# A two-layer graph network on one core: source one-hots by ScalarE and VectorE in three of seven chunks, and one gathered bucket of seven instead of two

## The chip, the cores and the metric

One core of a Trainium2 chip runs the whole program. The metric is the device time of one execution in microseconds (us). Below, PE is TensorE's matmul path, PEld its weight load, DVE is VectorE, ACT is ScalarE, POOL is GpSimd and SP is SyncE, whose queue issues most of the plain DMAs.

## What is computed

There are 6250 nodes with 128 channels and 200,000 edges (`src`, `dst`), sorted by `dst`. Two attention layers follow each other, and each adds its result to its input and normalizes the rows:

```python
hij = concat([h[src], h[dst]], axis=-1)                       # layer 0
exp_e = exp(leaky_relu(hij @ w, 0.2) @ a)
out = segment_sum(h[src] * exp_e / segment_sum(exp_e, src)[src], dst)
x = layernorm(x + out)

s = leaky(H_s[:, src] + H_t[:, dst]); s = exp(s - max(s))     # layer 1, 4 heads
agg = segment_sum(s / (segment_sum(s, src)[src] + 1e-8) * H[dst], src)
x = layernorm(x + elu(agg + x @ residual_projection))
```

## The kernel before

**Buckets.** The nodes are cut into 49 blocks of 128. Every edge lies in one of 49 x 49 buckets, by its destination's block j and its source's block i, and a bucket has 128 slots. For a bucket the kernel keeps, slot by slot, the edge's source and destination inside their blocks: as columns (`cols`, slots on partitions) and as rows in DRAM (`rows_jm`, `rows_im`). A row of numbers that is copied to all 128 partitions and compared with the partition's number gives a one-hot matrix, nodes by slots; a matmul with it as the weights reads a block's table rows out into the slots (a gather). The transposed matrix, slots by nodes, sums slots back into nodes. Buckets are worked off in chunks of seven, so a row of 49 buckets has seven chunks, c = 0 to 6. The engines run freely, each in the order of its own queue as the program writes it; they wait for each other through buffers and data.

**Stage A, `score_edges`, up to about 1520 us.** For each destination block j: while row j is scored, the slots of row j+3 are found (`find_slots`, a generator whose steps are interleaved by `find_more`, one step of each running generator after each chunk). `score_chunk` (L817) does one chunk. SP fetches the number rows of chunk k+3 (L806). DVE makes the one-hots of chunk k+2 (`one_hot`, L813, both kinds in one instruction). PE gathers the tables of both ends in 42 matmuls (L834) into PSUM tiles named `u` of three buckets each, of which there are four. DVE turns each bucket into one score per edge (L844, two instructions for a bucket). Then PE turns the seven one-hots of the sources (L850), and ACT copies the result from PSUM to `oh` (L852). Ten such `oh` tiles are kept: one row later, after chunk 1, `sums` (L790) uses the row's seven for the softmax's denominators. After chunk 6, ACT and DVE take the row's exponentials and split them into bf16 parts (`split3`, L476 to L480), in turns. Of `find_slots`, the prediction names the one-hot of the high digits (L666, read by PE at L673), the running counts (L682 and L684, which also use `u` tiles), the comparison at L723, the slot matmuls (L736), and L745, the first DVE step after them.

**Loading the ids.** `load_ids` (L599) reads the window of the edge list in which block j's edges lie, in two indirect DMAs from POOL's queue, whose row numbers are column j of `window_row`. One call stands after chunk 3 of each row, and eleven in the start-up. `split_ids` (L620) takes a group of seven of them apart on DVE.

**Stage B, the first part of `bucketed`, about 1540 to 2510 us.** It forms layer 0's sums, a row j at a time, each chunk in two groups of three and four buckets (`CUT`). Of a group's buckets, PE gathers those for which `by_dma` says no (L1289, three bf16 matmuls a bucket, from an exact split into three bf16 parts), and ACT copies them from PSUM (L1298). The others, the last `GP` of each chunk's seven in all rows but the first, come by indirect DMA from a table in DRAM (L1106, `Gathers`, POOL's queue, five chunks ahead). DVE makes the weighted one-hots (L1304, one a bucket), and PE sums them (L1320, f32; the profile counts two for each). `OneHots` fetches and converts (L1002) only the rows that PE needs. Each time seven rows are done, `nodes` is started: it normalizes these seven blocks and makes layer 1's tables, interleaved with the groups. Its writes (L1200, L1201) stand in SP's queue before later fetches of rows.

**Stage C, the second part, about 2535 to 3580 us.** It does the same for layer 1, a source block i at a time: L1367 and L1368 are the scores of the next row, L1419 the gather on PE, L1106 again the indirect DMA, L1436 the weighting (DVE, one instruction for the part from PSUM and one for the part from the DMA), L1443 the one-hots (DVE), L1457 the sums (PE). The scores need the one-hots of all seven buckets, so nothing is left out of their making. A tail (residual, elu, normalization, output) ends the program.

A second routine, `any_edges`, serves inputs that do not fit the slots; it does not run here.

Of the kernel before, what the change touches and what calls it, by code (L numbers as in the profile page):

```python
# [10 lines left out]
BF16 = mybir.dt.bfloat16  # L11
I32 = mybir.dt.int32
AF = mybir.ActivationFunctionType
OP = mybir.AluOpType
AX = mybir.AxisListType

P = 128
# [456 lines left out]
def split3(nc, pool, hi, mid, lo, v, shape, name):  # L474

    nc.scalar.activation(hi, v, AF.Copy)  # L476
    r = pool.tile(shape, F32, name=name)
    nc.vector.tensor_tensor(r, v, hi, op=OP.subtract)
    nc.scalar.activation(mid, r, AF.Copy)
    nc.vector.tensor_tensor(lo, r, mid, op=OP.subtract)  # L480


def score_edges(tc, keep, x, src, dst, w0, a0, rows_jm, rows_im):
# [4 lines left out]
    nc = tc.nc  # L488
    N, C = x.shape
    (E,) = src.shape  # L490
    NB = -(-N // P)
# [6 lines left out]
    CH = 7  # L498
    chunks = [(c, min(c + CH, NB)) for c in range(0, NB, CH)]
    NC = len(chunks)  # L500
    AHEAD = 3


    BEGIN, FIRST = (7, 16, 25, 35), 23
# [6 lines left out]
    cols = keep.tile([P, NB, 2, NB], BF16, name="cols")  # L511
# [3 lines left out]
    with ExitStack() as pools:  # L515
        fc = pools.enter_context(tc.tile_pool(name="fc", bufs=1))
# [3 lines left out]
        fa = pools.enter_context(tc.tile_pool(name="fa", bufs=2))  # L520
        fb = pools.enter_context(tc.tile_pool(name="fb", bufs=2, space=bass.MemoryType.PSUM))
        ft = pools.enter_context(tc.tile_pool(name="ft", bufs=2, space=bass.MemoryType.PSUM))
# [3 lines left out]
        nc.gpsimd.iota(iota_i, pattern=[[1, P]], base=1, channel_multiplier=0)  # L526
        iota_1 = fc.tile([P, P], BF16, name="iota_1")
        nc.vector.tensor_copy(iota_1, iota_i)
        part_i = fc.tile([P, 1], I32, name="part_i")
        nc.gpsimd.iota(part_i, pattern=[[0, 1]], base=0, channel_multiplier=1)  # L530
        part_f = fc.tile([P, 1], F32, name="part_f")
# [8 lines left out]
        ident_b = fc.tile([P, P], BF16, name="ident_b")  # L540
# [21 lines left out]
        window_row = fc.tile([P, NB], I32, name="window_row")  # L562
# [36 lines left out]
        def load_ids():  # L599

            j = len(loaded_ids)
            if j == NB:
                return
            b = next(b for b, (c0, c1) in enumerate(id_groups) if c0 <= j < c1)
            c0, c1 = id_groups[b]
            if j == c0:
                ids[b] = [fi.tile([P, CH, WT], I32, name=f"ids{k}") for k in range(2)]
            for to, flat in zip(ids[b], (src, dst)):
                if j == NB - 1:
                    nc.sync.dma_start(to[:, j - c0, :], flat[E - WT * P :].rearrange("(p t) -> p t", t=WT))  # L610
                    continue
                nc.gpsimd.indirect_dma_start(  # L612
                    out=to[:, j - c0, :],
                    out_offset=None,
                    in_=flat[: NR * WT].rearrange("(r t) -> r t", t=WT),
                    in_offset=bass.IndirectOffsetOnAxis(ap=window_row[:, j : j + 1], axis=0),
                )
            loaded_ids.append(j)

# [167 lines left out]
        def sums(j, ohs, ex3):  # L787
            dp = fb.tile([P, 3 * NB], F32, name="sm")
            for i in range(NB):
                nc.tensor.matmul(dp[:, 3 * i : 3 * i + 3], ohs[i // CH][:, i % CH, :], ex3[:, i, :], start=True, stop=True)  # L790
            if j == 0:
                nc.vector.tensor_copy(den, dp)
            else:
                nc.vector.tensor_tensor(den, den, dp, op=OP.add)
# [4 lines left out]
        def fetch(k):  # L799
            if k < len(order):  # L800
                j, c = order[k]
                c0, c1 = chunks[c]
                loaded[k] = ra.tile([P, 2, CH, P], BF16, name="rows")
                for w in range(2):
                    r = rows_jm[j, w, c0:c1].rearrange("r s -> (r s)")
                    nc.sync.dma_start(  # L806
                        loaded[k][:, w, : c1 - c0].rearrange(flat2), r[None, :].to_broadcast([P, (c1 - c0) * P])
                    )

        def one_hot(k):  # L810
            if k < len(order):
                rows = loaded[k].rearrange("p w i s -> p (w i s)")
                nc.vector.tensor_scalar(rows, rows, part_f, None, op0=OP.is_equal)  # L813

        state = {}

        def score_chunk(k):  # L817
            j, c = order[k]
            if c == 0:
                state["acc"] = wa.tile([P, NB], F32, name="acc")  # L820
                state["ohs"] = []
            acc, ohs = state["acc"], state["ohs"]
            fetch(k + 3)
            one_hot(k + 2)
            rows = loaded.pop(k)
            c0, c1 = chunks[c]
            for i0 in range(c0, c1, 3):
                n = min(3, c1 - i0)
                u = pa[0].tile([P, 512], F32, name="u")[:, : 3 * CX].rearrange("p (n c) -> p n c", c=CX)
                for d in range(n):  # L830
                    i = i0 + d
                    for w, b in ((0, i), (1, j)):
                        for s in range(3):
                            nc.tensor.matmul(  # L834
                                u[:, d, :],
                                rows[:, w, i - c0, :],
                                pq3[:, b, w, s, :],
                                start=(w == 0 and s == 0),
                                stop=(w == 1 and s == 2),
                            )  # L840
                for d in range(n):
                    i = i0 + d
                    junk = wa.tile([P, CX], BF16, name="junk")
                    nc.vector.scalar_tensor_tensor(  # L844
                        junk, u[:, d, :], 0.0, a_ext, op0=OP.max, op1=OP.mult, accum_out=acc[:, i : i + 1]
                    )

            tp = ft.tile([P, CH, P], BF16, name="tp")
            for i in range(c0, c1):
                nc.tensor.transpose(tp[:, i - c0, :], rows[:, 0, i - c0, :], ident_b)  # L850
            oh = woh.tile([P, CH, P], BF16, name="oh")
            nc.scalar.activation(oh[:, : c1 - c0], tp[:, : c1 - c0], AF.Copy)  # L852
            ohs.append(oh)
            if c == 1 and "late" in state:
                sums(*state["late"])
            if c + 1 == NC:
                nc.scalar.activation(ex[:, j, :], acc, AF.Exp, scale=1.0 - ALPHA)
                ex3 = wa.tile([P, NB, 3], BF16, name="ex3")
                split3(nc, wa, ex3[:, :, 0], ex3[:, :, 1], ex3[:, :, 2], ex[:, j, :], [P, NB], "exr")
                state["late"] = (j, ohs, ex3)  # L860
# [3 lines left out]
        with tc.tile_pool(name="n0", bufs=3) as n0:  # L864

            def tables(b, xt):
                mm = pa[0].tile([P, 512], F32, name="u")[:, : 2 * CX].rearrange("p (w c) -> p w c", c=CX)
                nc.tensor.matmul(mm, xt, w0_sb, start=True, stop=True)
                split3(nc, n0, pq3[:, b, :, 0, :], pq3[:, b, :, 1, :], pq3[:, b, :, 2, :], mm, [P, 2, CX], "pqr")
# [17 lines left out]
            for b in range(NB):  # L887
# [3 lines left out]
                tp = pa[0].tile([P, 512], F32, name="u")[:, :P]  # L891
# [23 lines left out]
            tables(*turned.pop(0))  # L915
            assert begun == len(BEGIN) == AHEAD + 1

        for k in range(scored, len(order)):
            j, c = order[k]
            if c == 0 and j > 0:  # L920
                if j + AHEAD < NB:
                    finding.append(find_slots(j + AHEAD))
                elif j + 1 == NB:
                    finding.append(check_slots())
            score_chunk(k)
            find_more()
            if c == 3:
                load_ids()
# [6 lines left out]
def bucketed(ctx, tc, x, w1, al, ar, wr, out, cols, ex, den, rows_jm, rows_im):  # L935
    nc = tc.nc
# [4 lines left out]
    NB = -(-N // P)  # L941
    LAST = N - (NB - 1) * P
    CD = C + H
    CH = 7
# [114 lines left out]


    CUT = 3
    GP = 2
    BY_PE = CH - GP
    assert NB % CH == 0

# [7 lines left out]
    class Gathers:  # L1073


        def __init__(self, pool, table, which, ahead, width):
            self.pool, self.table, self.ahead, self.width = pool, table, ahead, width
            base_i = consts.tile([P, NC, GP], I32, name=f"base_i{which}")
            nc.gpsimd.iota(base_i, pattern=[[CH * P, NC], [P, GP]], base=BY_PE * P, channel_multiplier=0)
            base = consts.tile([P, NC, GP], F32, name=f"base{which}")  # L1080
            nc.vector.tensor_copy(base, base_i)

            self.ids = consts.tile([P, NB, NC, GP], I32, name=f"ids{which}")
            for q in range(GP):
                if which == 0:
# [588 lines left out]
```

## Time and profile before

| | |
|---|---|
| median of 10 runs | 3642.73 us (3636.48 to 3644.98) |
| the profiled execution | 3637.54 us, of which the profile's span is 3635.7 us |
| PE busy | 3365.6 us, 93% |
| PEld busy | 3226.2 us, 89% |
| DVE busy | 3175.4 us, 87% |
| ACT busy | 2027.8 us, 56% |
| POOL busy | 1500.7 us, 41% |
| mean granted TensorE clock | 0.969 |

A group's line gives the line of code, the engine, the operation, the tiles (out<-in), the shape, the count, the busy time, the mean duration in ns and the idle time before it. Durations of neighbours overlap by some 0.1 us, so that the distance from one start to the next is the better price. A timeline's line gives the start and the duration in us and merges like instructions that follow each other; a bracket is the engine's idle time and who ended it.

### The profile page before, as it was taken

The page shows a single profiled execution, that of the slowest core. Times are in us where ns is not written, and L with a number is a line of the kernel's source. Part 1 is how long each engine was busy: PE and PEld are TensorE (multiplying, and loading weights), DVE is VectorE, ACT ScalarE, POOL GpSimd, SP SyncE. Part 2 cuts the span into 40 slices and gives each one's busy share as a digit, 9 for nine tenths or more (in the row PEclk, how much of TensorE's full clock was granted, in tenths as well). Part 3 has the DMA queues.
Part 4 walks back from the last instruction along what each step waited for, and adds up shares of the span by engine and source line. Part 5 has one row for each costly group of instructions (what it writes and reads, how often), then busy time and mean ns, then how long its engine had stood idle before and what let it go on. Part 6 is the DMA issues. An engine that isn't in the chain of part 4 may idle for free.

```text
span 3635.7 us, 125212 instructions
## 1 busy us (share of the span) xinstructions
PE 3365.6 (93%) x50166; PEld 3226.2 (89%) x50166; DVE 3175.4 (87%) x11723; ACT 2027.8 (56%) x3036; POOL 1500.7 (41%) x1474
## 2 busy tenths in 40 slices
PE   4699999999999999799999999997999999999996
PEld 3598989898989899788988988987999999999996
DVE  5588888888888888798888888887999999999997
ACT  4556666666666666343333333334666666666665
POOL 4001010101000000157766766764567676777771
PEclk6799999999999999899999999998999999999998
DMA  2133343333444433454544544445666666666672
GB/s 62 37 118 121 121 117 122 116 124 118 121 116 121 116 118 122 145 124 115 118 113 113 117 113 114 117 114 144 188 201 189 201 200 197 196 199 203 191 198 82
DMA packets 348224, 496.41 MB, mean 137 GB/s; under 512 B 65806, under 2 KB 325347, under 8 KB 347634
## 3 DMA queue, kind: packets, MB, share of 16 engines
q1 hardware_dynamic: 296520, 393.32, 36.6%
q0 software_dynamic: 46992, 94.52, 11.5%
q8 instruction: 399, 6.54, 0.7%
q14 instruction: 191, 1.56, 0.2%
q10 hardware_dynamic: 4122, 0.47, 0.1%
HBM read 472.71 MB, written 15.39 MB: 134 GB/s over the span
## 4 chain that ended last, share of the span: by engine, by line
PE 72%; DVE 17%; ACT 5%; issue 3%; DMA 3%; another core or an unknown queue 0%; POOL 0%; SPq 0%; ACTq 0%; DVEq 0%; POOLq 0%
PE u L1457 15%; PE oj L1320 14%; PE u L834 14%; PE he L1419 8%; PE ye L1289 7%; DVE junk L844 3%; PE sm L736 2%; PE tp L850 2%; DVE rows L813 2%; DMA rows<-rows_jm 2%; PE u L684 2%; DVE vst L711 2%; PE sp L1368 1%; PE u L682 1%; PE sm L673 1%
## 5 line engine op out<-in xcount | busy, mean ns | idle before, releaser
L834 PE MATMUL u<-pq,rows 128*128 128x130 bf16 x14406 | 911.7, 221 | 63.7 <-DVE junk L844 56.8
L834 PEld LDWEIGHTS <-rows 128*128 128x128 bf16 x14406 | 854.0, 98 | 77.2 <-issue 68.1
L1106 POOL DMA_INDIRECT rows_g<-h_d,ids x672 | 716.6, 1066 | 346.0 <-DVE z L1436 175.8
L1106 POOL DMA_INDIRECT rows_g<-y_d,ids x672 | 667.2, 993 | 289.4 <-PE oj L1320 114.7
L1304 DVE TENSOR_SCALAR oh<-iota_b,dsts,ex 128x128 f32<-128x128 bf16 x2401 | 667.4, 361 | 70.0 <-ACT dsts L1282 45.4
L1457 PE MATMUL u<-z,oh 128*128 128x132 f32 x4802 | 701.0, 286 | 0.0
L844 DVE SCALAR_TENSOR_TENSOR junk<-u,a_ext 128x130 bf16<-128x130 f32 x2401 | 546.1, 289 | 89.8 <-PE u L834 88.0
L1457 PEld LDWEIGHTS u<-z,oh 128*128 128x128 f32 x4802 | 592.5, 190 | 0.8
L852 ACT ACTIVATE oh<-tp 128x896 bf16<-128x896 bf16 x343 | 314.3, 916 | 447.5 <-PE tp L850 445.7
L1298 ACT ACTIVATE yc<-ye 128x384 f32<-128x384 f32 (+2 forms) x686 | 298.2, 438 | 476.1 <-PE ye L1289 461.4
L1320 PE MATMUL oj<-yc,oh 128*128 128x128 f32 x3458 | 544.1, 289 | 13.0 <-ACT yc L1298 10.7
L1320 PEld LDWEIGHTS oj<-yc,oh 128*128 128x128 f32 x3458 | 448.1, 195 | 16.2 <-ACT yc L1298 12.4
L1289 PE MATMUL ye<-y,rows 128*128 128x128 bf16 x5187 | 409.6, 222 | 51.3 <-DVE rows L1002 50.4
L1443 DVE TENSOR_TENSOR oh<-iota_b,cols 128x384 f32<-128x384 bf16 (+2 forms) x693 | 421.1, 608 | 0.0
L1419 PE MATMUL he<-h,rows 128*128 128x132 bf16 x5187 | 417.3, 221 | 0.0
L1289 PEld LDWEIGHTS <-rows 128*128 128x128 bf16 x5187 | 354.2, 99 | 69.2 <-DVE rows L1002 32.5
L612 POOL DMA_INDIRECT ids<-in_src_dram,window_row x48 | 57.4, 1195 | 763.0 <-DVE tmp L632 730.1
L1419 PEld LDWEIGHTS <-rows 128*128 128x128 bf16 x5187 | 358.7, 98 | 10.2
L1436 DVE TENSOR_TENSOR z<-he,w 128x396 f32<-128x396 f32 (+2 forms) x693 | 339.4, 490 | 24.8 <-PE he L1419 24.0
L997 ACT ACTIVATE rows<-rows,minus_p 128x896 bf16<-128x896 bf16 x336 | 346.3, 1031 | 24.9 <-DMA rows<-rows_im 16.2
L998 ACT ACTIVATE rows<-rows 128x896 bf16<-128x896 bf16 x336 | 319.3, 950 | 10.6
L1002 DVE TENSOR_SCALAR rows<-rows,part_f 128x896 bf16<-128x896 bf16 (+1 forms) x693 | 286.6, 414 | 9.6 <-DMA rows<-rows_jm 5.1
(209 smaller groups left out, 4648.1 us busy)
## 6 DMA issues: line engine op xcount, KB each, us to landing
rows<-rows_jm SPq DMA_DIRECT2D x693, 224.0 KB
rows<-rows_im SPq DMA_DIRECT2D x686, 224.0 KB
rows<-rows_jm SPq DMA_DIRECT2D x336, 160.0 KB
rows_g<-y_d,ids POOLq DMA_INDIRECT x672
rows_g<-h_d,ids POOLq DMA_INDIRECT x672
h_d<-hx SPq DMA_DIRECT2D x6, 462.0 KB
xc<-in_x_dram SPq DMA_DIRECT2D x6, 448.0 KB
x_sb<-in_x_dram POOLq DMA_DIRECT2D x6, 448.0 KB
```

Of the source, the lines that this page charges most:

```text
L834: nc.tensor.matmul(u[:, d, :], rows[:, w, i - c0, :], pq3[:, b, w, s, :], start=(w == 0 and s == 0), stop=(w == 1 and s == 2),)
L844: nc.vector.scalar_tensor_tensor(junk, u[:, d, :], 0.0, a_ext, op0=OP.max, op1=OP.mult, accum_out=acc[:, i : i + 1])
L997: nc.scalar.activation(rows, rows, AF.Square, bias=minus_p)
L998: nc.scalar.activation(rows, rows, AF.Relu, bias=1.0, scale=-1.0)
L1106: nc.gpsimd.indirect_dma_start(out=t[:, q, :], out_offset=None, in_=self.table[:, :], in_offset=bass.IndirectOffsetOnAxis(ap=self.ids[:, r ...
L1289: nc.tensor.matmul(ye[:, k, :], oh[:, i0 + k - c0, :], y3[:, i0 + k, s, :], start=(s == 0), stop=(s == 2))
L1304: nc.vector.tensor_scalar(oh[:, k, :], iota_b, dsts[0][:, i : i + 1], ex[:, j, i : i + 1], op0=OP.is_equal, op1=OP.mult,)
L1320: nc.tensor.matmul(outs[j], oh[:, k, :], values[k], start=(i == 0), stop=(i == NB - 1))
L1419: nc.tensor.matmul(he[:, k, :], oh[:, j0 + k - c0, :], h3[:, j0 + k, s].rearrange("p h e -> p (h e)"), start=(s == 0), stop=(s == 2),)
L1436: nc.vector.tensor_tensor(z[:, a:b].rearrange("p n (h e) -> p n h e", h=H), rows.rearrange("p n (h e) -> p n h e", h=H), weights[i][:, j0 ...
L1443: nc.vector.tensor_tensor(oh[:, :n], iota_b[:, None, :].to_broadcast([P, n, P]), cols[:, j0 : j0 + n, 0, i : i + 1].to_broadcast([P, n, P] ...
L1457: nc.tensor.matmul(aggs[i], oh[:, k, :], z[:, k, :], start=(j == 0), stop=(j == NB - 1))
```

## The change

In stage A, chunks 1, 3 and 5 of each row no longer turn the sources' one-hots on PE. ACT spreads each slot's number from `cols` over 128 columns of `oh`, and after the next chunk's scores DVE compares `oh` in place with a row of the numbers 0 to 127 (`iota_0`, made once). The other four chunks stay as they were. `load_ids` copies its column of `window_row` to a tile of its own on DVE, from a pool of two, and the indirect DMAs read that. In stages B and C, `GP` goes from 2 to 1: of the seven buckets of a chunk one comes by DMA, and six are gathered by PE.

```diff
+    BY_DVE = (1, 3, 5)
...
+        iota_0 = fc.tile([P, P], BF16, name="iota_0")
+        nc.vector.tensor_scalar(iota_0, iota_1, -1.0, None, op0=OP.add)
...
+            row = fa.tile([P, 1], I32, name="row")
+            nc.vector.tensor_copy(row, window_row[:, j : j + 1])
...
-                    in_offset=bass.IndirectOffsetOnAxis(ap=window_row[:, j : j + 1], axis=0),
+                    in_offset=bass.IndirectOffsetOnAxis(ap=row, axis=0),
...
-            tp = ft.tile([P, CH, P], BF16, name="tp")
-            for i in range(c0, c1):
-                nc.tensor.transpose(tp[:, i - c0, :], rows[:, 0, i - c0, :], ident_b)
+            for oh_d in state.pop("spread", []):
+                nc.vector.tensor_tensor(oh_d, oh_d, iota_0[:, None, :].to_broadcast([P, CH, P]), op=OP.is_equal)
             oh = woh.tile([P, CH, P], BF16, name="oh")
-            nc.scalar.activation(oh[:, : c1 - c0], tp[:, : c1 - c0], AF.Copy)
+            if c in BY_DVE:
+                nc.scalar.activation(oh, cols[:, j, 0, c0:c1, None].to_broadcast([P, CH, P]), AF.Copy)
+                state["spread"] = [oh]
+            else:
+                tp = ft.tile([P, CH, P], BF16, name="tp")
+                for i in range(c0, c1):
+                    nc.tensor.transpose(tp[:, i - c0, :], rows[:, 0, i - c0, :], ident_b)
+                nc.scalar.activation(oh, tp, AF.Copy)
...
-    GP = 2
+    GP = 1
```

More of the change, by code (lines that the diff above doesn't have):

```diff
@@ L501, in score_edges @@
     AHEAD = 3
+    assert NB % CH == 0
+    BY_DVE = (1, 3, 5)
     BEGIN, FIRST = (7, 16, 25, 35), 23
```

## The prediction

> **What bounds the kernel now.** The page shows PE busiest, but the three stages differ, so I cut windows over one steady row of each stage (A, B, C) and over a row of B in which `nodes` runs (third line). The columns are PE, PEld, DVE, ACT, POOL, then the granted clock.
>
> ```profile
> 735.00:762.50 27.50, 26.57 (x509) 25.29 (x505) 24.19 (x123) 18.05 (x22) 0.00 (x0) 1.00 0.39 121
> 1612.83:1630.38 17.55, 17.55 (x207) 17.39 (x205) 15.50 (x57) 6.25 (x15) 13.43 (x14) 1.00 0.55 116
> 1714.00:1739.00 25.00, 21.32 (x225) 20.59 (x225) 22.68 (x78) 7.86 (x19) 15.41 (x16) 0.93 0.39 94
> 2583.92:2605.17 21.25, 21.25 (x308) 20.76 (x306) 20.65 (x52) 14.03 (x17) 14.97 (x15) 1.00 0.70 198
> ```
>
> In steady rows of B and C, PE has no idle time at all, and DVE has some (2 us and 0.6 us). In A both have gaps. The rows' lengths come from the starts of L1322 and L1459: 17.55 us in B (24 to 25 in two rows of seven, where `nodes` runs), 21.2 in C; in A, from L857, 27.5 (32 in one row of seven).
>
> PE's timeline in B and C shows the two groups of a chunk beside each other: nine gather matmuls for three buckets, six for two.
>
> ```profile
> 1612.63 0.67 PE L1289 MATMUL ye<-y,rows 128*128 128x128 bf16 x9
> 1613.13 0.89 PE L1320 MATMUL oj<-yc,oh 128*128 128x128 f32 x6
> 1613.86 0.50 PE L1289 MATMUL ye<-y,rows 128*128 128x128 bf16 x6
> 1614.19 0.66 PE L1320 MATMUL oj<-yc,oh 128*128 128x128 f32 x4
> ...
> 2583.72 0.69 PE L1419 MATMUL he<-h,rows 128*128 128x132 bf16 x9
> 2584.25 0.89 PE L1457 MATMUL u<-z,oh 128*128 128x132 f32 x6
> 2584.98 0.52 PE L1419 MATMUL he<-h,rows 128*128 128x132 bf16 x6
> 2585.33 0.17 PE L1367 MATMUL sp<-st,rows 128*128 128x12 bf16 x1
> ```
>
> From start to next start, nine take 0.50 us in B and 0.53 in C, six take 0.33 and 0.35. A third bucket thus costs PE 0.17 us and 0.18 us, and the work behind it starts that much later.
>
> For A, the timeline of one row (PE works about a chunk ahead of DVE).
>
> ```profile
> 746.61 0.55 PE L850 MATMUL tp<-ident_b,rows 128*128 128x128 bf16 x7
> 747.00 2.60 PE L834 MATMUL u<-pq,rows 128*128 128x130 bf16 x42
> 748.60 0.21 DVE L478 TENSOR_TENSOR exr<-ex,ex 128x49 f32<-128x49 f32 x1 [1.20 <-ACT ex L476]
> 751.86 1.55 PE L834 MATMUL u<-pq,rows 128*128 128x130 bf16 x24 [0.78 <-DVE junk L844]
> 756.89 1.09 DVE L666 TENSOR_TENSOR soh<-spread,iota 128x1800 bf16<-128x1800 bf16 x1
> 757.89 0.68 DVE L813 TENSOR_SCALAR rows<-rows,part_f 128x1792 bf16<-128x1792 bf16 x1
> 759.98 1.35 DVE L723 TENSOR_TENSOR at<-spread,iota 128x2304 bf16<-128x2304 bf16 x1
> 761.25 0.68 DVE L813 TENSOR_SCALAR rows<-rows,part_f 128x1792 bf16<-128x1792 bf16 x1
> 765.69 0.29 DVE L844 SCALAR_TENSOR_TENSOR junk<-u,a_ext 128x130 bf16<-128x130 f32 x1 [0.40 <-PE u L834]
> ```
>
> The row's path changes engine. DVE works without a gap from L745 (749.3) through chunks 0 to 3; PE waits for it at 751.86, for L666 at 758.0, and at 762.62, where the second count tile needs the first `u` of chunk 3, freed by its third L844 (762.56). From there PE sets the pace through chunks 4, 5 and 6, and DVE waits (0.40 and 0.31 us in chunk 4, 0.64 and 0.31 in chunk 6). Chunk 6's copy, the exponentials and `split3` close the circle, with DVE idle for 1.20 and 0.35 us.
>
> **B and C: one more bucket on PE.** 48 rows x 7 chunks = 336 chunks, each with three more matmuls. B: 336 x 0.17 = 57 us; C: 336 x 0.18 = 60 us. In C no wait of PE can take it, and DVE's work does not change: L1436 at 264 elements twice costs 420 + 418 ns, and at 396 (561 ns) plus 132 (about 277, by the line through 264 and 396) the same 838. I take 60, from 55 (1008 matmuls at 55 ns from start to start, the distance within L850's seven) to 61. In B, PE waits in the `nodes` rows, 2.75 us in the one and 4.9 us in the next, at seven places in the stage. Those waits end by DVE's chain and by SP's late rows, which PE's queue reaches with more work still in hand: I take 1.4 of the 2.4 us that two rows add as hidden, 10 us in all, with ends 0 and 17. Longer conversions (380 to about 414 ns at L1002) add 1 us where DVE is late. B: +48, from 37 to 58. ACT's copies grow from 382 to 490 ns, beside 11 idle us a row.
>
> What the halved gathers give back is POOL's: 336 x 1.07 us in C, 336 x 0.99 in B. No PE instruction waits for a gathered row in these rows, so that is worth nothing. At the two changes of stage one L1089 goes (0.7 us each): -1.
>
> The Trainium skill, "TensorE: Matmul & The Clock Gate", section "Back-to-back issue gap", gives about 81 ns a matmul for a stream of weight loads and matmuls at 128 columns. By it the 2016 matmuls would cost an estimated 163 us; the trace's nine against six say 57 + 60, and the trace decides.
>
> **A: three chunks without turning.** Seven turns and the way to the next start cost 0.39 us (746.61 to 747.00), 1.17 a row. The comparison has 896 elements; of its kind are L666 (1800, next start 1.00 us later) and L723 (2304, 1.27 us): 0.54 ns an element, so 0.52 us (0.61 if durations, 1088 and 1353 ns, are extended instead), 1.56 a row. Where do they lie?
> - Chunk 1's comparison stands in chunk 2, inside DVE's gapless stretch: +0.52 on the path. The turns of chunks 1 and 3 stand where PE waits for DVE anyway: nothing back.
> - Chunk 3's comparison stands in chunk 4, where DVE idles 0.7 us, and chunk 5's in front of `split3`'s wait of 1.2 us: hidden. Without these covers each costs 0.52. A comparison waits for ACT's spread, which ACT was given a chunk earlier; what queues behind it is the next L723, L694 or `split3`.
> - Chunk 5's turns stand on PE's stretch: -0.39.
>
> So a row grows by 0.13 us, 45 rows by 6 us. The last three rows find no slots and are PE's alone (21.1 to 24.2 us): -1.1 each, -3. ACT's spread should take about 0.95 us by L716 and L660 (2113 ns for 2304, 1696 for 1800), against 0.92 at L852, and no longer waits for PE; ACT has 9 idle us a row. The copy in `load_ids` (about 0.1 us, as L707's distance) falls into chunk 4's gap. It also waits until the gathers of two blocks before have read their tile, with all of DVE queued behind; a row lies between them. And it ties POOL to DVE's order: POOL ran up to 195 us ahead, and now a window's numbers come in a row's time. In the steady part they are still asked for a row or more before `split_ids`. In the start-up, the seventh is asked for one block before, and two DMA issues (0.94 + 0.30 each) and the landing would hold up DVE: +2, from 0 to 4. A: +5, from -15 (chunk 3's turns returned as well) to +25 (a second comparison exposed, or more stretches at a low clock: over the `nodes` row above 0.93 was granted, which loses 1.75 of 25 us, and gaps on PE decide it).
>
> **Sum.** 5 + 48 + 60 - 1 = +112. The profiled execution took 3637.5, so 3749.5; its median stands 5.2 higher: 3755.
>
> **Rivals.**
> 1. PE bounds A after all, and all turns return: 1029 x 55.5 ns = 57 us. For it: PE 26.6 of 27.5 us busy. Against: PE's waits for DVE above. -55 in place of +5, with 48, 60 and -1 as above: 3695. Chance 0.08.
> 2. All three comparisons land on DVE's path: 3 x 0.52 - 0.39 = 1.17 us a row, +53 in place of +5: 3803. For it: DVE would hold 25.8 of 27.6 us; against: the idle places named. Chance 0.07.
> 3. The other side: DVE, not PE, paces B and C (PE's ends are modelled, DVE holds 20.65 of 21.25 us in C). The added matmuls are free as long as they stay under DVE's row, and A gives back 55: 3587. It decides if PE's row after stays at 17.6 and 21.2 us. Against it: DVE has gaps there and PE none. Chance 0.04.
>
> My case has the rest, 0.81. Its ends: -15 + 37 + 55 - 1 = +76 and 25 + 58 + 61 - 1 = +143, so 3719 to 3786. To leave out no more than 2 in 10, the range also takes in rival 1: 3692 to 3786. About 0.2% (7 us) can be told from no change. Faster comes from rival 3 alone (0.04), no change needs partial forms of it (0.01), the rest is slower.
>
> **What would show it.** B's steady row at 18.7 us, C's at 22.4, A's between 27.4 and 28; L1289 and L1419 at 6195 matmuls each; L850 at 1372; L1106 at 336 twice. I am wrong if steady rows of B or C grow by less than 0.8 us, or A's shrink by over 0.4.

## The result and the profile after

The changed kernel takes 3732.17 us (median of 8 runs, 3728.59 to 3734.86), the kernel before 3642.46 us beside it (28 runs): ratio 1.0247, interval 1.0238 to 1.0256. It is slower by 90 us; the forecast was 3755, within 3692 to 3786. The profiled executions differ by as much: the span is 3726.4 us against 3635.7.

Cut at the first and last start of L857, L1322 and L1459 (now L870, L1335 and L1472, the lines that end a row), the two spans divide so:

| stretch | before, us | after, us | difference | forecast |
|---|---|---|---|---|
| up to the first row of A, and A | 184.5 + 1334.2 | 180.6 + 1327.7 | -10.4 | +5 |
| B | 933.3 | 979.5 | +46.2 | +48 |
| C | 1015.8 | 1066.8 | +51.0 | +60 |
| A to B, B to C, the tail | 59.0 + 51.6 + 57.3 | 61.2 + 50.7 + 59.8 | +3.8 | -1 |

The windows of the kernel after, in the columns shown before (PE, PEld, DVE, ACT, POOL, granted clock): a steady row of A, one of B, a row of B in which `nodes` runs, and a steady row of C.

```profile
735.00:762.40 27.40, 25.56 (x488) 24.14 (x486) 25.77 (x125) 18.02 (x21) 2.11 (x3) 1.00 0.43 123
1600.00:1618.70 18.70, 18.70 (x226) 18.53 (x226) 15.49 (x58) 6.99 (x16) 6.59 (x8) 1.00 0.34 100
1712.00:1737.40 25.40, 21.89 (x239) 21.17 (x238) 22.71 (x76) 8.47 (x19) 7.20 (x7) 0.93 0.30 91
2699.96:2722.29 22.33, 22.33 (x328) 22.00 (x327) 21.10 (x52) 14.03 (x16) 8.05 (x7) 1.00 0.61 167
```

Steady rows of B are 18.7 us (17.55 before) and of C 22.33 (21.22 before), and the view shows no idle time of PE in them, as before. POOL's share has halved, and nothing has become shorter for it. In A, DVE now holds more of the row than PE, which has given up 1.0 us.

PE's timeline of the kernel after shows the price of the added bucket. Both groups of a chunk now have nine gather matmuls.

```profile
1600.05 0.67 PE L1302 MATMUL ye<-y,rows 128*128 128x128 bf16 x9
1600.55 0.89 PE L1333 MATMUL oj<-yc,oh 128*128 128x128 f32 x6
1601.28 0.39 PE L1333 MATMUL oj<-rows_g,oh 128*128 128x128 f32 x2
1601.50 0.67 PE L1302 MATMUL ye<-y,rows 128*128 128x128 bf16 x9
...
2700.26 0.69 PE L1432 MATMUL he<-h,rows 128*128 128x132 bf16 x9
2700.79 1.11 PE L1470 MATMUL u<-z,oh 128*128 128x132 f32 x8
```

The second group's gather takes 0.50 us in B and 0.53 in C (start to next start), where six took 0.33 and mostly 0.35. The page's groups of the kernel after have the counts named beforehand (6195 for L1432 too; L865 copies 196 x 7 = 1372 turns):

```profile
L1119 POOL DMA_INDIRECT rows_g<-h_d,ids x336 | 384.6, 1145 | 724.2 <-DVE z L1449 687.7
L1302 PE MATMUL ye<-y,rows 128*128 128x128 bf16 x6195 | 466.3, 221 | 48.1 <-DVE rows L1015 47.0
L865 ACT ACTIVATE oh<-tp 128x896 bf16<-128x896 bf16 x196 | 179.7, 917 | 385.2 <-PE tp L864 385.2
```

### The profile page after: what moved, and what is told of

The parts are those of the page before. It is cut to its first block, busy times and chain, and to the rows that moved or that the text cites. A ratio compares the mean times of both kernels' runs of the same rounds, so it can differ in the third digit from the quotient of the medians.

```text
span 3726.4 us, 126093 instructions
## 1 busy us (share of the span) xinstructions
PE 3427.3 (92%) x51153; PEld 3289.9 (88%) x51153; DVE 3273.9 (88%) x11918; ACT 2062.5 (55%) x3036; POOL 825.5 (22%) x802
## 4 chain that ended last, share of the span: by engine, by line
PE 74%; DVE 15%; ACT 5%; issue 3%; DMA 2%; another core or an unknown queue 0%; SPq 0%; POOL 0%; ACTq 0%; POOLq 0%; DVEq 0%
PE u L1470 16%; PE oj L1333 14%; PE u L841 14%; PE he L1432 10%; PE ye L1302 8%; DVE junk L851 3%; PE sm L743 2%; PE u L691 2%; DVE rows L820 2%; PE sp L1381 2%; DVE vst L718 2%; PE sm L680 2%; PE u L689 1%; PE sp L1380 1%; DVE oh L1317 1%
## 5 line engine op out<-in xcount | busy, mean ns | idle before, releaser
L841 PEld LDWEIGHTS <-rows 128*128 128x128 bf16 x14406 | 862.3, 98 | 95.2 <-issue 86.0
L1333 PE MATMUL oj<-yc,oh 128*128 128x128 f32 x4130 | 618.3, 286 | 10.2 <-ACT yc L1311 9.0
L1311 ACT ACTIVATE yc<-ye 128x384 f32<-128x384 f32 (+1 forms) x686 | 334.7, 491 | 496.1 <-PE ye L1302 489.0
L1119 POOL DMA_INDIRECT rows_g<-h_d,ids x336 | 384.6, 1145 | 724.2 <-DVE z L1449 687.7
L1333 PEld LDWEIGHTS oj<-yc,oh 128*128 128x128 f32 x4130 | 522.8, 194 | 13.2 <-ACT yc L1311 10.9
L1302 PE MATMUL ye<-y,rows 128*128 128x128 bf16 x6195 | 466.3, 221 | 48.1 <-DVE rows L1015 47.0
L1119 POOL DMA_INDIRECT rows_g<-y_d,ids x336 | 326.9, 973 | 676.6 <-PE oj L1333 567.8
L1432 PE MATMUL he<-h,rows 128*128 128x132 bf16 x6195 | 475.7, 221 | 0.0
L1302 PEld LDWEIGHTS <-rows 128*128 128x128 bf16 x6195 | 411.2, 99 | 65.7 <-DVE rows L1015 28.9
L1449 DVE TENSOR_TENSOR z<-he,w 128x396 f32<-128x396 f32 (+1 forms) x693 | 389.8, 562 | 56.0 <-PE he L1432 39.5
L1432 PEld LDWEIGHTS <-rows 128*128 128x128 bf16 x6195 | 417.3, 97 | 10.2
L865 ACT ACTIVATE oh<-tp 128x896 bf16<-128x896 bf16 x196 | 179.7, 917 | 385.2 <-PE tp L864 385.2
```

What stands on the lines that cost most here:

```text
L841: nc.tensor.matmul(u[:, d, :], rows[:, w, i - c0, :], pq3[:, b, w, s, :], start=(w == 0 and s == 0), stop=(w == 1 and s == 2),)
L1119: nc.gpsimd.indirect_dma_start(out=t[:, q, :], out_offset=None, in_=self.table[:, :], in_offset=bass.IndirectOffsetOnAxis(ap=self.ids[:, r ...
L1302: nc.tensor.matmul(ye[:, k, :], oh[:, i0 + k - c0, :], y3[:, i0 + k, s, :], start=(s == 0), stop=(s == 2))
L1311: nc.scalar.activation(yc[:, :m], ye[:, :m], AF.Copy)
L1333: nc.tensor.matmul(outs[j], oh[:, k, :], values[k], start=(i == 0), stop=(i == NB - 1))
L1432: nc.tensor.matmul(he[:, k, :], oh[:, j0 + k - c0, :], h3[:, j0 + k, s].rearrange("p h e -> p (h e)"), start=(s == 0), stop=(s == 2),)
```

## The experiments

They ran on three chips, four kernels on each (13, 8 and 14 by the records), and there the kernel before took 4211.94, 4210.36 and 4148.86 us instead of 3642: the same program, with 125212 instructions in both profiles. Which chip the first measurement used isn't recorded. So each kernel is compared with the kernel before on its own chip, and the first question, what the parts of the change cost, got a second one beside it: what made the kernel before 570 us longer.

### The two halves of the change

Here `GP = 1` alone, and beside it everything else with `GP = 2` (`BY_DVE = (1, 3, 5)` and the row copy).

```diff
-    GP = 2
+    GP = 1
```

> The kernel before with GP = 1 alone. Theory (PE paces stages B and C, so a third bucket costs what its matmuls cost; stage A is a separate account): +46 us in B and +51 in C, as in the changed kernel's rows, some 3739 us in all, with B's steady row at 18.7 us and C's at 22.3, and stage A as before. Rival (part of B's and C's loss comes from stage A's side of the change, or hides there): a total that differs from 3739 by more than 6 us.

> The changed kernel with GP back at 2: stage A's part and the copy in load_ids alone. Theory (A's account is its own, and small): stage A's rows at 27.4 us as in the changed kernel, B and C as before, 3632 to 3638 us in all, that is 5 to 11 us less than before. Rival (the turns were PE's bound in A, and something of the changed kernel's other part hid it): 3590 to 3610 us.

`gp1_only` took 3832.11 us (5 runs; 3739 were expected), ratio 0.9101 (0.9087 to 0.9116): far faster. `turns_only` took 4129.86, ratio 0.9814 (0.9795 to 0.9833). The half that made the kernel slower in the first measurement makes it faster here. Its own stages are nevertheless those of the kernel after: B 978.6 us and C 1066.8, rows of 18.7 and 22.3. It is the kernel with two gathered buckets that differs: in `turns_only` B takes 1111.7 us and C 1291.3, against 933.3 and 1015.8 in the first profile. So the price of the third bucket on PE stands, and on these chips two gathers a chunk cost something that the first trace did not hold.

In A, `turns_only` has the kernel after's steady row where no ids are loaded (27.43 us). Its early part also shows what the row copy is worth here: rows with 12 or 14 id gathers in one burst, 42 to 47 us long in `gp1_only`, are 31 to 32 us long in `turns_only`, where the copy ties the gathers to DVE's order, one pair a row. The part ahead of A tells the same: in the trace of `gp1_only` 42 id gathers are issued there and it takes 217.1 us, in `turns_only` 22 and 180.6.

### One chunk at a time

The kernel before with the comparison for one chunk alone.

```diff
+    BY_DVE = (1,)        # chunk1;  (5,) in chunk5,  (3,) in chunk3
```

> The kernel before with chunk 1 alone by spread and comparison, and without the copy in load_ids. Theory (chunk 1's comparison stands in DVE's gapless stretch, its turns where PE waits anyway): a steady row of A grows by 0.54 us, 45 of them by 24 us; the last rows give back 1: some 3665 us. Rival (each chunk's turns come back in equal parts and each comparison costs equally): a third of the whole part's change, some -3 us, 3639.

> The kernel before with chunk 5 alone by spread and comparison, and without the copy in load_ids. Theory (its turns stand on PE's stretch, its comparison in front of split3's wait, where DVE idles): a steady row of A shrinks by 0.39 us, 45 of them by 17.5 us, with the last rows 18.5: some 3624 us, with DVE's wait for the exponentials shorter by 0.5 us and nothing later. Rival (equal parts): -3 us, 3639. Second rival (the wait of split3 only moves behind the comparison, so that the comparison costs in full): 3642 + 45 x 0.15 = 3649.

> The kernel before with the comparison for chunk 3 alone. Theory from the trace after: chunk 3's turns return 0.27 us a row and its comparison, in chunk 4, lies in an idle time of DVE: steady row 27.28 in place of 27.55 us, 45 rows, -12 us in A. The forecast's step (turns of chunk 3 return nothing): 27.55, 0 us. A rival (the comparison is exposed): 27.8 or more, +12 to +23 us. Ratio 0.9967, 1.000 or 1.005 against 3642 us; stages B and C as before.

`chunk1` took 4236.28 us, ratio 1.0053 (1.0035 to 1.0071); `chunk5` 4190.10, ratio 0.9946 (0.993 to 0.9961); `chunk3` 4202.96, ratio 0.9976 (0.9962 to 0.9989). The rows near the end of A, where no ids are loaded, give the sharper reading: row 40 is 28.09 us in `chunk1`, 27.16 in `chunk5` and 27.56 in `chunk3`, against 27.55 in the kernel before. So +0.54, -0.39 and 0.01. The first two are the forecast's steps. The third is too (turns of chunk 3: nothing back; comparison in chunk 4: hidden), and against the theory formed from the trace after, which gave them 0.27. Over the whole of A `chunk1` costs more than 45 times its step: 1424.5 us against 1387.0 in `gp1_only`, whose A is that of the kernel before. Thirteen of its rows have a granted clock of 0.94 and take 29.6 to 29.9 us; in the first profile only the one long row in seven falls below 1.00. `chunk3`'s ratio is below 1, but its stage A is as long as in the kernel before on that chip (1384.8 us against 1384.6), so the change of A did not bring it; the runs don't say what did.

Alone, then, the three add up to +0.16 us a row. Together they gave -0.12. The three traces show where the difference arises: in PE's wait before the second count tile, L682 of the kernel before. In `chunk3`:

```profile
1409.05 0.37 PE L687 MATMUL u<-soh,down_to 128*128 128x500 bf16 x1 [0.41 <-DVE junk L849]
```

In `chunk1`:

```profile
1445.38 0.37 PE L687 MATMUL u<-soh,down_to 128*128 128x500 bf16 x1 [0.55 <-DVE junk L849]
```

In the kernel after:

```profile
757.67 0.37 PE L689 MATMUL u<-soh,down_to 128*128 128x500 bf16 x1 [0.68 <-ACT up L698]
```

With one chunk changed, the tile waits for the first `u` of chunk 3, which DVE frees with its third product. With all of them changed, the tile waits on ACT's semaphore instead of DVE's, for the instruction that empties the first count tile: by this it has been given that tile's buffer of the four. `turns_only`, the same A on another chip, has the same wait of 0.68 us. The first count can start earlier, because chunk 3's turns no longer stand before it, and so ACT is done sooner than DVE. The second count tile then starts 14.88 us into row 40, against 15.15 in `chunk1`, 0.27 us earlier, and what follows on PE with it. That is 45 x 0.27 = 12 us that the parts do not show one by one.

### What the kernel before spends 570 us on here

The kernel before, once more for its trace, and a version that issues only the first of the two gathers (the second's place holds ones, so its sums lack those rows):

```diff
-                for q in range(GP):
+                for q in range(1):
```

> The kernel before itself, once more, for its trace beside the experiments. If it takes about 4212 us again, as in the first four experiments: rows of B near 22 us (18.7 with one gathered bucket), of C near 27 us (22.3), and gaps of over 0.3 us inside runs of like matmuls that no wait explains, some 0.6 us behind the issue of an indirect DMA by POOL (theory: the issues hold up PE). A rival: the rows are longer because the gathers land later; then PE's gaps have a releaser, DMA. If it takes about 3642 us: rows of 27.5, 17.55 and 21.2 us, and no such gaps.

> As before, but in stages B and C the second gather of each chunk is not issued (its place in the tile holds ones), so POOL issues half as many DMAs and PE's work is unchanged. Where the kernel before takes about 4212 us: if the issues hold up PE, B's row goes from 22 to about 17.6 us and C's from 27 to about 21.2, B at about 933 us and C at about 1016, some 440 us less in all, ratio about 0.895; if the third PE bucket or the bytes mattered, less than half of that. Where the kernel before takes about 3642 us: B and C within 5 us of 933 and 1016, ratio 1.00, by the forecast's step that no PE instruction waits for a gathered row; the rival that DVE or the DMA queues set B's and C's rows would give 2% or more.

`before_again` took 4206.44 us (one run, span 4204.6). Against the first profile A is longer by 50.4 us, B by 186.8, C by 274.3, the part ahead of A by 30.7 and the two changes of stage by 26.7; the tail is the same 57.3. `half_gathers` took 3731.80 us, ratio 0.8858 (0.8835 to 0.8881): 479 us less. Its B takes 929.3 us and its C 1018.3, within 4 us of the first profile. A row of C in `before_again`:

```profile
3668.47:3695.68 27.21, 23.98 (x308) 22.71 (x306) 21.20 (x52) 14.14 (x16) 14.77 (x14) 0.94 0.54 154
```

and in `half_gathers`:

```profile
3290.53:3311.76 21.23, 21.23 (x308) 20.77 (x306) 20.64 (x52) 14.14 (x17) 8.09 (x8) 1.00 0.60 175
```

The counts are the same 308 matmuls. With both gathers PE has 3.2 us of gaps in the row, and its busy time is 2.75 us longer as well. The clock granted in this row is 0.94, but that is the smaller part: from 3000 to 3500 us it is 1.00, rows take 25.8 to 28.4 us all the same, and PE is busy 427 us for 5627 matmuls, 76 ns each, against 70 in the C of `half_gathers`. So some of the standing still lies inside what the view counts as busy. What ended PE's gaps over 300 us of C, in `before_again` (engine, line, releaser: us in total, times, longest):

```profile
PE u L1401 <- DVE m L1396: 16.3, 11, 1.6
PE u L1457 <- issue: 9.9, 32, 0.5
PE he L1419 <- issue: 5.2, 17, 0.5
PE sp L1368 <- issue: 4.5, 10, 0.5
PE sp L1367 <- issue: 3.5, 7, 0.5
```

In the same length of C of `half_gathers` the view has one wait, of 0.8 us. "Issue" means that the profile shows nothing that PE waited for: 66 such gaps, 23 us. The 16.3 us at L1401 are a wait for DVE's chain of scores (0.8 us in the first profile), and DVE itself waits for PE longer there, some 50 us against 6. No DMA is among the releasers, so the rival of gathers that land late falls. One of the gaps, in the middle of a run of like matmuls, from `before_again`'s timeline:

```profile
3310.35 0.94 POOL L1106 DMA_INDIRECT rows_g<-h_d,ids  x1 [0.30 <-issue]
...
3311.31 0.17 PE L1368 MATMUL sp<-st,rows 128*128 128x12 bf16 x1 [0.47 <-issue]
```

This gap begins inside the second issue of a pair and ends with it. Between the first gather of B and the last of C the trace has 321 gaps of over 0.2 us that the view puts down to issue; the first profile has none. Of the 321, 317 end behind a gather that was issued within 0.6 us of the end of the one before, and 4 behind a gather issued after a pause, although a quarter of the time lies behind these. Closeness alone doesn't bring the gaps: in the first profile 629 of the 663 gathers of B follow within 0.4 us. POOL's own issue isn't longer (1051 ns a gather in C, 1066 in the first profile). The Trainium skill, "DMA: Bandwidth & Descriptors", section "SWDGE vs HWDGE vs iDMA", says that GpSimd writes the descriptors of such a DMA itself, to rings in SBUF, and that VectorE locks it out of that memory during its 2-port perf mode. That would lengthen POOL's issue, which isn't seen; on PE standing still it says nothing.

### Closeness, or rows?

A fill of 256 elements by POOL between the two gathers, and two gathers of 64 partitions each (the other rows hold ones, so its sums lack them):

```diff
+                    if q:
+                        nc.gpsimd.memset(self.filler, 0.0)          # spaced_gathers
...
-                        out=t[:, q, :],
+                        out=t[:64, q, :],                           # narrow_gathers, its ids too
```

> The kernel before with a fill of a scratch tile (256 elements, about 0.35 us) by POOL between the two gathers of a chunk in B and C; both gathers stay. Theory 1: PE stalls because the second issue follows the first at once (0.3 us). Then PE's unexplained gaps go; POOL needs 2.05 us of issue and about 1.1 us of the rest a chunk, so B stays near 22 to 23 us a row, but C falls from 27 to 22 to 23.5: 160 to 240 us less, ratio 0.94 to 0.96. Theory 2: it is the number of issues or of fetched rows in a chunk: the gaps stay, C at 27 or longer, ratio 1.00 to 1.03. If the kernel before takes 3642 us: B longer by up to 5 us a row, C by up to 2.

> The kernel before with both gathers of a chunk in B and C issued for 64 of the 128 partitions each; the other rows hold ones. The issues stay two a chunk and as close; the fetched rows and the packets are those of one gather. Theory of the issue: gaps as before, B near 22 us, C near 26 to 27, ratio 0.97 to 1.00. Theory of the rows (packets, descriptors): as with one gather, B 17.6, C 21.2, ratio 0.89. If the issue itself becomes shorter (by the nearest row, 1.05 us for 128 rows, between 0.5 and 1.05), a mixture. If the kernel before takes 3642 us: ratio 1.00.

`spaced_gathers` took 4096.28 us, ratio 0.9877 (0.9854 to 0.9901); `narrow_gathers` 4138.96, ratio 0.998 (0.997 to 0.9989). Over 300 us of C, the gaps of `spaced_gathers` that are put down to issue, those of over 0.5 us in total:

```profile
PE he L1422 <- issue: 5.9, 21, 0.4
PE u L1404 <- issue: 1.4, 1, 1.4
PE u L1460 <- issue: 1.1, 4, 0.3
PE sp L1370 <- issue: 0.8, 2, 0.4
```

and of `narrow_gathers`:

```profile
PE sp L1370 <- issue: 6.1, 11, 1.2
PE sp L1371 <- issue: 5.0, 8, 1.2
PE u L1460 <- issue: 4.6, 15, 0.5
PE he L1422 <- issue: 3.5, 12, 0.4
PE u L1404 <- issue: 0.9, 1, 0.9
```

By the ratio, half the rows bring 10 us, where half the issues brought 479; the bytes that are fetched are not the main cause. The packets remain: POOL's queue moved 49.8 MB in place of 94.5, but the same 46992 packets as in the kernel before, where `half_gathers` has 25488. So this run does not tell the number of packets from the number of issues.

Space between the two issues (0.5 us in place of 0.3) brings C to 1182.7 us, against 1253.7 in `narrow_gathers`, and the gaps put down to issue, over the whole of C, to 31 us against 81. (The kernel before took 60 us less on this chip than on the one of `before_again`, so these two are set against each other rather than against that trace.) In B, where POOL was expected to have no room for the fill, they are 53 us against 31, and B takes 1088.4 us (1080.7 in `narrow_gathers`). The ratio falls short of the 0.94 to 0.96 expected: 0.5 us does not end the gaps (rows of C are 22.3 to 27.6 us). The fill also stands only inside a chunk: 138 of the 329 chunks of C still issue their first gather within 0.4 us of the chunk before. The runs spread from 4064 to 4109 us, and the profiled one is the shortest.

What is shown is this: on these chips the gaps are there with two gathers a chunk and gone with one. That the second gather holds up PE because it follows closely is likely by where the gaps lie and by C with the fill; it is not shown, and the number of issues or of packets in a chunk remains as a rival. How a gather holds up PE, and why the first measurement was free of it, whether by its chip or by something else that differed then, stays open. Nothing that was run tells apart the engines' instruction supply, a shared bus and the semaphores.

### The changed kernel on such a chip

> The changed kernel itself on the chips of the experiments, where the kernel before took 4210 us. Theory: with one gather a chunk there are no gaps of PE behind POOL's second gather, so it takes what it took before, 3732 us (3722 to 3745), rows 27.4, 18.7 and 22.3 us, ratio 0.886. Rival: these chips are slower in everything: 4210 x 1.0247 = 4314. If the kernel before takes 3642 us: ratio 1.0247.

`after_again` took 3748.20 us, where the kernel before took 4148.86: ratio 0.9032 (0.9016 to 0.9048). B takes 978.7 us and C 1066.8, as in the first profile of it, to 1 us; A's 1336.7 are 9.0 more, in rows in which ids are loaded. The rival of chips that are slower in everything falls with it. The change is a loss of 2.5% in the first measurement and a gain of 9.7% on this chip.

### Other chunks

Chunks 3, 4 and 5 with `GP = 2`, and chunks 4 and 5 with `GP = 1`, both with the row copy:

```diff
+    BY_DVE = (3, 4, 5)   # late_chunks;  (4, 5) and GP = 1 in late_two_gp1
```

> Gathered buckets two as before, the row copy in, and the comparisons for chunks 3, 4 and 5 in place of 1, 3 and 5: none of them in DVE's gapless stretch. Theory: the turns of chunks 3, 4 and 5 return 0.27 + 0.39 + 0.39 us and the comparisons lie in DVE's idle times of chunks 4 to 6: steady row 26.5 us, A 47 us less than before, -3.9 at the start, ratio about 0.986 against 3642 us. Rival: DVE's idle time holds two comparisons and not three (0.7 + 1.2 us in all against 1.56): row 26.9 to 27.1, 20 to 30 us less. Where the kernel before takes about 4212 us, the row copy, which spreads the gathers of A over its rows, gives another 60 to 80 us, and B and C stay as before there, ratio about 0.97.

> A version that should beat both kernels on these chips: one gathered bucket and the row copy as in the change, but the comparisons for chunks 4 and 5 alone, whose turns stand where PE sets A's pace (0.28 + 0.39 us a row by the runs with chunks 3 to 5 and chunk 5), and none inside DVE's gapless stretch. Steady row 26.8 to 26.9 us against 27.43 in the changed kernel: A 25 us less, 3700 to 3712 us against 3732, ratio to the kernel before 0.88. Rival: chunk 4's comparison is exposed where chunk 3's turns stay: row 27.2, 3720 us.

`late_chunks` took 4129.28 us, ratio 0.9803 (0.978 to 0.9826). Row 40 is 26.88 us, of which DVE is busy 25.61. That is -0.67 us, the rival's figure and not the theory's -1.05: DVE's idle time is down to 1.3 us and the third comparison shows. While ids are loaded its rows are 28.1 us here. `late_two_gp1` took 3734.91 us, ratio 0.9002 (0.8986 to 0.9018), and its row 40 is the shortest of all (PE, PEld, DVE, ACT, POOL, clock):

```profile
1306.83:1333.60 26.77, 25.85 (x495) 24.55 (x493) 25.11 (x123) 17.90 (x22) 0.00 (x0) 1.00 0.38 125
```

It beats both kernels on this chip: 13 us under the changed kernel there, all of it in A (1323.9 us against 1336.7). About 25 were expected; while ids are loaded, its rows are 27.5 and not 26.8 us. Where two gathers cost nothing, as in the first measurement, the best of the tried parts would by these rows be chunks 4 and 5 with two gathered buckets. That was not run.

## Why the prediction held, point by point

**B, +48: measured +46.2.** The steady row grew by 1.17 us (7 x 0.17), and the two `nodes` rows, by 0.9 together, hid 1.4 of 2.4 us as taken. The estimate of 163 us for B and C from the Trainium skill ("TensorE: Matmul & The Clock Gate", "Back-to-back issue gap") was too high: B and C grew by 97 us. Where nothing was hidden, an added matmul cost 56 ns in B (0.50 us for nine) and 59 in C (0.53), against the page's 81.

**C, +60: measured +51.0.** The price of a group was right (0.176 us in the mean of 20 rows, taken as 0.18; seven times a row 1.23), but a row grew by 1.11. "In C no wait of PE can take it" was wrong by one wait. In the kernel before, one group of six in each row stands ahead of L1401, the transposition of the maximum that DVE's chain behind the scores forms (L1396), and there the way to the next start is 0.46 us and more in place of 0.35:

```profile
2958.86 0.52 PE L1419 MATMUL he<-h,rows 128*128 128x132 bf16 x6
2958.91 0.36 DVE L1396 TENSOR_REDUCE m<-score 128x1 f32<-128x196 f32 x1
2959.32 0.27 PE L1401 MATMUL u<-ident,m 128*1 128x128 f32 x1
```

and after:

```profile
3015.52 0.36 DVE L1409 TENSOR_REDUCE m<-score 128x1 f32<-128x196 f32 x1
3015.61 0.69 PE L1432 MATMUL he<-h,rows 128*128 128x132 bf16 x9
3016.13 0.27 PE L1414 MATMUL u<-ident,m 128*1 128x128 f32 x1
```

Before, L1401 starts 0.06 us after the maximum's end at 48 of its 49 places; after, 0.26 us behind it at 47, with nine gathers of 0.53 us in front like all the others. The longer gather fills what was a wait of 0.11 us and more, 0.17 in the mean of 48 rows: 8 of the 9 us. The window over one row couldn't show it, because the modelled 0.52 us of the six covers the wait and PE's total comes out full. The distances from start to start show it.

**A, +5: measured -10.4.** Chunk 1's comparison on DVE's path (+0.54 us, taken as 0.52), chunk 5's turns on PE's (-0.39) and chunk 3's nothing are each confirmed by its own run. What failed is their sum. I took "the turns of chunks 1 and 3: nothing back" from a trace in which the second count tile waits for DVE; in the kernel after it has another buffer and waits for ACT, 0.27 us a row earlier, 12 us. Against that, three rows at a granted clock of 0.94, of the kind that the upper end had allowed for, take 29.0 to 29.3 us. The start is 3.9 us shorter where +2 was taken, as a cost of the copy. On the three chips it takes 214.5 to 217.1 us in the eight profiles without the copy and 180.6 to 182.5 in the four with it, whatever else differs; so the copy, which leaves 22 of 42 id gathers in the start, is what shortens it there; in the first measurement it may be the same, which no run shows.

**Stage changes and the tail, -1: measured +3.8**, not explained by any run.

**The rivals.** In rival 1 all turns return: they do not, chunk 1 alone lengthens the row. In rival 2 three comparisons are exposed: one is, DVE's wait in front of `split3` fell from 1.20 to 0.66 us as its cover was used. Rival 3 decides at steady rows of 17.6 and 21.2 us: they are 18.7 and 22.3.

**The halved gathers, worth nothing.** This held in the first measurement, as far as a run elsewhere can show it: `half_gathers` has rows of 17.55 and 21.23 us, those of the kernel before with both gathers there. In the later runs the second gather cost 479 us in all (by `half_gathers`), and no row of the first trace shows it.

## What to carry to other kernels

Price a step that moves work to PE by the distance from start to start in a stage where PE never idles, and take these distances at every place of a row before calling it gapless: a busy time that comes out full can cover a short wait. Do not add the returns of single steps where buffers are handed round: two that return nothing alone can return something together. Where a kernel issues indirect DMAs from POOL in close pairs, measure it on more than one chip and at more than one time before deciding; here the sign of the change hangs on it.

## What the runs showed of the hardware

- The same program took 3642 us in the first measurement and 4212, 4210 and 4149 us on three chips, yet a steady row of C with single gathers there is 21.23 us, as with pairs in the first measurement (21.22).
- On those chips, with two indirect DMAs a chunk issued 0.3 us apart, PE stands still, mostly for 0.3 to 0.7 us at a time, without a wait that the trace shows; with one a chunk it does not. C's row is 26 to 28 us with pairs and 21.2 with single ones. In the first measurement the same pairs brought no such gap.
- There, a row of A with a burst of 12 or 14 id gathers took 42 to 48 us, where the same row took 32 in the first measurement.
- PE's busy time can cover a short wait: in C a wait of 0.17 us a row showed only in the distances from start to start.
